# Layers L0 and L1 of a graph network: the sums of a group of edges are taken up one step later, and the ends of a block of nodes spread over the steps after it

## The chip, the cores and the metric

The kernel runs on one core of a Trainium2 chip. The metric is the device time of one execution in microseconds; the profile beside it is of one execution of the same program. TensorE is called PE here (its weight loads PEld), VectorE DVE, ScalarE ACT, GpSimd POOL, and SyncE SP; SP issues most of the plain transfers.

## What is computed

Four graph layers follow each other over the same 6,250 nodes of 256 features and 100,000 edges, which are sorted by their target node. Before each layer the node rows go through a layer norm and a ReLU, and the layer's result is added to the node rows. The two that the change touches, cut to what matters:

```python
def _L0_gnn_ref(x, edge_index, ...):          # attention over edges, 8 heads of 32
    Qh, Kh, Vh = (x @ Wq + bq), (x @ Wk + bk), (x @ Wv + bv)      # each [N, 8, 32]
    s = einsum('nhc,nhc->nh', Qh, Kh) / sqrt(32)
    alpha = leaky_relu(s[src] + s[dst], 0.2)                      # edges and self loops
    e = exp(alpha - segment_max(alpha, dst)[dst])
    a = e / segment_sum(e, dst)[dst]
    attn = segment_sum(Vh[src] * a[:, :, None], dst)
    h = batch_norm(x + attn @ Wo + bo)
    return batch_norm(h + relu(h @ W1 + b1) @ W2 + b2)

def _L1_gnn_ref(x, rbf, dists, edge_index, ...):   # a filter for each edge
    W = (rbf @ W_r2m.T + b_r2m) * (0.5 * (cos(dists * (PI / 5)) + 1))[:, None]
    h = (x @ W_n2m.T + b_n2m) @ W_lin1.T
    agg = segment_sum(h[src] * W, dst)
    return (agg @ W_lin2.T + b_lin2) @ W_m2n.T

h = relu(layernorm(x)); x = x + L0(h)
h = relu(layernorm(x)); x = x + L1(h, edge_attr_32, edge_weight)
h = relu(layernorm(x)); x = x + L2(h, edge_attr_128)
h = relu(layernorm(x)); x = x + L3(h)
```

## The kernel before

Nodes are kept in 49 blocks of 128 (`NB`). Edges come in 98 groups (`G`) of 8 tiles (`J`) of 128, so a group holds 1,024 edges. Each layer first writes a table of node rows to memory (`vt` for L0, `ht1` for L1, `xt2` and `xt3` for L2 and L3); then a loop over the groups gathers, for every edge, the row of its source node. One gather is an indirect transfer of 128 rows, issued by POOL (`gather`, line 130), 8 for each group.

A group's edges end in a window of 128 target nodes, which starts 64 nodes (`HW`) after that of the group before. The segment sum over a group is done on PE: for each of the 8 tiles a one-hot matrix (edge by node of the window, made by DVE from `iota` and `rel`) is multiplied with the weighted rows, and the 8 products are summed in one PSUM tile, `ps_S` (`sum_tiles`, line 681). A block of nodes is touched by up to four windows; `blocks_done(g)` names the block whose last window is that of group g, so it is block b at g = 2b + 2, every second step, and block 48 at the last group, 97.

The four layers are four such loops. Between L0 and L1 stand L0's feed-forward part and the table of L1, from 1226 to 1495 us, without gathers. A gather of L1 needs the whole of `ht1`, and one of L2 the whole of `xt2`.

The order of the work is written out by hand in the parts under `tc.manual_schedule()`: each engine runs its instructions in the order in which the code names them, and an instruction that waits holds up all behind it on its engine.

*L0, step g of the loop at line 818.* The gathers of a group go into one of 6 places in `xbuf` (`NV`) and wait only until PE has summed the group that lay there 6 groups before; the first four groups' gathers are issued ahead of the loop. SP loads `drow` for group g + 2, and `v`, the block's own value rows. Then:

- `sum_block` (line 699) moves the windows of the block that was finished by group g - 1 into place, by 2 to 4 matmuls with shifted unit matrices, in `ps_T` (one buffer). `project0` (line 800) multiplies the block finished by group g - 2 with Wo, in `ps_B` (two buffers).
- `logits0` on DVE (lines 771, 123, 773) adds the target's score to the gathered scores; ACT makes the exponentials (lines 774, 775). `one_hot_t` (line 748, DVE) makes `to`, the one-hot of the next group with nodes on the partitions, from `drow`, and PE uses it in `of_dst` (line 763) to fetch the next group's target scores into `ps_A`. Line 836 (DVE) weights the gathered rows.
- `attn0` (lines 781 to 786, DVE) adds the self loop and divides, for the block in `ps_T`.
- `sum_window` (lines 681 and 691) sums the group on PE, and ACT copies the sum to `ws` at once.
- `turn0` (lines 792, 794) transposes the block on PE, and ACT copies it to `mt`. `one_hot0` (line 754, DVE) makes the next group's 8 one-hots. `residual0` (lines 808, 810, DVE) adds the projected block and takes its statistics for the batch norm, which needs all blocks.

*L1, step g of the loop at line 1005.* The gathers go into one of 12 places in `big` (`NH`). `filters` (line 980, PE) makes the edge filters in three `ps_A` buffers, line 1026 (DVE) multiplies them into the gathered rows, PE sums the window, now with features on the partitions, and DVE and ACT add it to `agg` (lines 1056, 1057) at the end of the same step. Lines 1031 and 1032 (DVE) work out an edge term for L2. For a finished block, line 1015 (PE) projects its 128 columns of `agg`, `out1` (lines 992 to 995, DVE, with the statistics in lines 145 and 146 and ACT's square root in line 126) adds it to the node rows and norms them, line 1022 transposes, ACT applies the ReLU (line 1038), line 1041 multiplies with the weights of L2's table, and lines 1047 to 1049 write the row of `xt2`. Here `ps_B` and `ps_C` have one buffer each, and `ps_S` two.

## Time and profile before

| What | us |
|---|---|
| median of 6 runs (lowest, highest) | 4501.55 (4499.86, 4505.31) |
| the profiled execution, and its span | 4501.5, 4499.7 |
| first gather of L0 to the end of its last | 180.7 to 1201.3 |
| feed-forward of L0 and table of L1 | 1226 to 1495 |
| first gather of L1 to the end of its last | 1495.3 to 2476.0 |
| gathers of L2 | 2495.8 to 3481.1 |
| gathers of L3 | 3502.0 to 4485.2 |
| PE, DVE, ACT, POOL busy over the span | 3079.4, 2103.6, 619.5, 3055.6 |

In the lines of the profile an instruction is named by its line in the kernel, its engine and its operation, and by its tiles (out<-in, with buffer numbers left out; `big<-ht` is a gather of L1, `xbuf<-vt` one of L0, `vg<-xt` one of L2 or L3). A line of the costliest groups ends with busy time and mean ns of one, and the idle time of the engine just before, with what ended it; "issue" is time in which the engine waited for nothing that the profile shows. A line of the waits has the sum in us, the number of times and the longest. A line of the timeline has start, duration and instruction, with the idle time before it in brackets. A line of the stretches has the length, then busy time and number of instructions of PE, PEld, DVE, ACT and POOL, the clock that PE was granted (1.00 is full speed), the share of the DMA engines in use and GB/s. A float32 matmul stands as two records, so 8 matmuls are x16.

### The profile page before, as it was taken

How to read it: one execution, taken by the hardware profiler on the slowest of the kernel's cores; microseconds unless marked ns; L12 is line 12 of the kernel's file. 1: busy time of each engine (PE TensorE's matmuls, PEld its weight loads, DVE VectorE, ACT ScalarE, POOL GpSimd, SP SyncE). 2: the span in 40 equal slices, each digit the busy share in tenths (PEclk: the TensorE clock that was granted, in tenths of full speed). 3: DMA queues.
4: the chain of work that ended last, by engine and by line, in shares of the span. 5: the costliest groups of instructions: out<-in, count | busy, mean ns of one | idle time of the engine just before them, and what ended most of it. 6: DMA issues, size and time to landing. Idle time of an engine off the chain costs nothing. (4 is left out here: it accounts for less than half of the span.)

```text
span 4499.7 us, 42030 instructions
## 1 busy us (share of the span) xinstructions
PE 3079.4 (68%) x12132; PEld 2392.3 (53%) x12133; DVE 2103.6 (47%) x6391; ACT 619.5 (14%) x1559; POOL 3055.6 (68%) x3215
## 2 busy tenths in 40 slices
PE   7788888888797556666666566666666556666655
PEld 4377777777645444555445344545454444444444
DVE  5476665566524566766667333333333222222222
ACT  3211010000124100000000122222222000000000
POOL 0377777777501677777777677777777677777776
PEclk9888888888898777777778788888888788787888
DMA  3365555555500344444444344444443333333333
GB/s 105 112 180 169 161 160 160 162 163 161 154 1 14 110 128 126 122 127 124 128 126 115 90 111 113 113 112 113 112 113 109 96 112 111 112 112 110 112 112 101
DMA packets 258740, 536.78 MB, mean 119 GB/s; under 512 B 65096, under 2 KB 144966, under 8 KB 258502
## 3 DMA queue, kind: packets, MB, share of 16 engines
q0 software_dynamic: 137984, 364.28, 28.6%
q1 hardware_dynamic: 107750, 156.85, 11.4%
q10 hardware_dynamic: 12768, 12.85, 0.9%
q8 instruction: 105, 1.72, 0.2%
q14 instruction: 133, 1.09, 0.1%
HBM read 504.57 MB, written 29.15 MB: 119 GB/s over the span
## 5 line engine op out<-in xcount | busy, mean ns | idle before, releaser
L130 POOL DMA_INDIRECT vg<-xt,src_i x1568 | 1488.7, 949 | 520.4 <-issue 486.7
L681 PE MATMUL ps_S<-vg,oh 128*128 128x258 f32 (+1 forms) x3136 | 986.0, 483 | 782.9 <-DMA vg<-xt,src_i 408.9
L681 PEld LDWEIGHTS ps_S<-vg,oh 128*128 128x128 f32 x3136 | 761.2, 249 | 999.9 <-issue 388.4
L130 POOL DMA_INDIRECT xbuf<-vt,src_i x784 | 782.0, 997 | 241.0 <-issue 211.2
L130 POOL DMA_INDIRECT big<-ht,src_i x784 | 742.1, 947 | 246.3 <-issue 183.8
L681 PE MATMUL ps_S<-oh,big 128*128 128x128 f32 x1568 | 320.9, 388 | 324.1 <-DVE big L1026 260.9
L1150 DVE TENSOR_SCALAR oh<-iota,rel 128x128 f32<-128x128 f32 x784 | 166.5, 302 | 742.5 <-PE ps_S L681 739.3
L681 PE MATMUL ps_S<-xbuf,oh 128*128 128x265 f32 x1568 | 489.8, 478 | 13.7 <-issue 13.4
L681 PEld LDWEIGHTS ps_S<-oh,big 128*128 128x128 f32 x1568 | 298.1, 292 | 354.7 <-DVE big L1026 235.2
L681 PEld LDWEIGHTS ps_S<-xbuf,oh 128*128 128x128 f32 x1568 | 369.5, 242 | 101.0 <-issue 17.4
L763 PE MATMUL ps_A<-scw,to 128*128 128x16 f32 x1568 | 223.7, 286 | 112.1 <-DVE to L748 111.9
L763 PEld LDWEIGHTS ps_A<-scw,to 128*128 128x128 f32 x1568 | 220.2, 223 | 131.2 <-issue 80.8
L1095 DVE TENSOR_SCALAR oh<-iota,rel,ex 128x128 f32<-128x128 f32 x784 | 215.1, 368 | 139.1 <-ACT ex L1092 139.1
L699 PE MATMUL ps_T<-ws,shifts 128*128 128x265 f32 (+2 forms) x1164 | 278.7, 382 | 0.0
L691 ACT ACTIVATE ws<-ps_S 128x265 f32<-128x265 f32 (+1 forms) x196 | 76.5, 390 | 1221.6 <-PE ps_S L681 1221.6
L699 PEld LDWEIGHTS ps_T<-ws,shifts 128*128 128x128 f32 x1164 | 220.8, 190 | 33.7
L836 DVE TENSOR_TENSOR xbuf<-xbuf,ps_E 128x2048 f32<-128x2048 f32 x98 | 223.6, 2282 | 23.7 <-ACT ps_E L774 23.7
L1026 DVE TENSOR_TENSOR big<-big,ps_A 128x384 f32<-128x384 f32 (+1 forms) x294 | 132.3, 505 | 215.2 <-DMA big<-ht,src_i 213.3
L980 PE MATMUL ps_A<-wr,rb 99*128 99x384 f32 (+1 forms) x588 | 215.7, 507 | 9.5 <-DMA rb<-in_rbf 9.5
L1088 DVE TENSOR_TENSOR al<-vg,te 128x8 f32<-128x8 f32 x98 | 16.4, 168 | 432.8 <-DMA vg<-xt,src_i 432.8
L988 DVE TENSOR_SCALAR oh<-iota,rel,cut 128x128 f32<-128x128 f32 x784 | 211.7, 362 | 0.0
L900 POOL TENSOR_TENSOR xbuf<-xbuf,bout 128x1024 f32<-128x1024 f32 (+1 forms) x13 | 29.0, 2228 | 257.5 <-ACT xn L898 250.7
(226 smaller groups left out, 3053.7 us busy)
## 6 DMA issues: line engine op xcount, KB each, us to landing
drow<-in_dst_row SPq DMA_DIRECT2D x98, 512.0 KB
ea<-in_edge_attr SPq DMA_DIRECT2D x98, 512.0 KB
vg<-xt,src_i POOLq DMA_INDIRECT x1568, 2.8
xbuf<-vt,src_i POOLq DMA_INDIRECT x784, 2.9
big<-ht,src_i POOLq DMA_INDIRECT x784, 2.5
rb<-in_rbf SPq DMA_DIRECT2D x196, 49.5 KB
vt<-row SPq DMA_DIRECT2D x49, 132.5 KB
xt<-row SPq DMA_DIRECT2D x49, 129.0 KB
```

Source lines behind the costliest of these rows:

```text
L130: return nc.gpsimd.indirect_dma_start(out=rows, out_offset=None, in_=table, in_offset=bass.IndirectOffsetOnAxis(ap=idx[:, j:j + 1], axis=0))
L681: m = wait_for(nc.tensor.matmul(s, l, r, start=j == 0, stop=j == len(pairs) - 1), made)
L691: nc.scalar.activation(ws, s, AF.Copy)
L699: nc.tensor.matmul(t, shift_by(s), sums[g], start=i == 0, stop=i == len(parts) - 1)
L763: nc.tensor.matmul(dgs[g][:, j, :], tos[g][:, j * P:(j + 1) * P], scw[:, g // 2, g % 2, :], start=True, stop=True)
L836: made_g = nc.vector.tensor_tensor(vals, vals, ex[:, :, :, None].to_broadcast([P, J, H, HD]), OP.mult)
L900: nc.gpsimd.tensor_tensor(x[:, b0:b1, :], x[:, b0:b1, :], w1["bout"][:, None, :].to_broadcast([P, b1 - b0, D]), OP.add)
L980: filtered[g] = nc.tensor.matmul(t, rbs[g][0:33 * n, g % 2, q, :], wr3[0:33 * n, 0:n, :], start=True, stop=True)
L988: nc.vector.tensor_scalar(ohs[g][:, j, :], iota, rel[:, c], w1["cut"][:, c], OP.is_equal, OP.mult)
L1026: made_g = nc.vector.tensor_tensor(hg[:, js, :], hg[:, js, :], t, OP.mult)
L1095: made_g = nc.vector.tensor_scalar(oh[:, j, :], iota, rel[:, g * J + j:g * J + j + 1], ex[:, j:j + 1], OP.is_equal, OP.mult)
L1150: made_g = nc.vector.tensor_scalar(oh[:, j, :], iota, rel[:, g * J + j:g * J + j + 1], None, OP.is_equal)
```

## The change

In both loops, ACT and DVE take up the PSUM sum of group g - 1 in step g (`wins` holds it until then) and no longer that of group g in the same step. The work of a finished block is spread: in L0 `sum_block` runs in the step after the block's last group, behind that step's sums, `attn0` and `turn0` one step later, the copy to `mt` and `project0` one after that, and `residual0` one more; before, `sum_block`, `attn0`, `turn0` and its copy stood in one step, `project0` and `residual0` in the next. In L1 the projection stands in the first step, `out1` and the transposes in the second, the ReLU and the row matmuls in the third, and the row's last addition and write in the fourth; before, the projection and `out1` stood in one step and all the rest in the next. L1's `filters` for the next group move ahead of the group's sums, and its one-hots ahead of the update of `agg` and of the edge term. L1's one-hots get a third buffer and `xn` a second. The loops run three steps more, in which only block work is left. No instruction is added or taken away beside the extra waits that follow from the order.

```diff
@@ -734,7 +734,8 @@
             place = ep.tile([P, G], F32, name="place", bufs=1)
             nc.gpsimd.iota(place, pattern=[[HW, G]], base=-OFF, channel_multiplier=1,
                            allow_small_or_imprecise_dtypes=True)
-            sums, drows, tos, dgs, ohs, mades, vs, ms, mts = {}, {}, {}, {}, {}, {}, {}, {}, {}
+            sums, drows, tos, dgs, ohs, vs, ms, mts = {}, {}, {}, {}, {}, {}, {}, {}
+            wins, blocks, turned, projected = {}, {}, {}, {}
 
             def loads0(g):
                 if g < G:
@@ -751,9 +752,8 @@
                 if g < G:
                     ohs[g] = ep.tile([P, J, P], F32, name="oh")
                     for j in range(J):
-                        mades[g] = nc.vector.tensor_scalar(ohs[g][:, j, :], iota,
-                                                           rel[:, g * J + j:g * J + j + 1],
-                                                           None, OP.is_equal)
+                        nc.vector.tensor_scalar(ohs[g][:, j, :], iota, rel[:, g * J + j:g * J + j + 1],
+                                                None, OP.is_equal)
 
             def of_dst(g):
 
@@ -790,8 +790,7 @@
                 t = ps("B", [P, 2, P])
                 for k in range(2):
                     nc.tensor.transpose(t[:, k, :], mf[:, k * P:(k + 1) * P], ident)
-                mts[b] = ep.tile([P, 2, P], F32, name="mt", bufs=1)
-                nc.scalar.activation(mts[b], t, AF.Copy)
+                return t
 
             def project0(b):
                 t = ps("B", [P, 2, P])
@@ -815,7 +814,7 @@
                 one_hot_t(0)
                 one_hot0(0)
                 of_dst(0)
-                for g in range(G + 2):
+                for g in range(G + 5):
                     vg = vrows[g % NV]
                     if AHEAD <= g < G:
                         rows0(g)
@@ -827,24 +826,34 @@
                         made(of1)
                     if g == 8:
                         made(of2)
-                    summed = [(b, sum_block(sums, b, VR)) for b in blocks_done(g - 1)]
-                    projected = [(b, project0(b)) for b in blocks_done(g - 2)]
                     if g < G:
                         ex = logits0(g)
                         one_hot_t(g + 1)
                         vals = vg[:, :, 0:D].rearrange("p j (h c) -> p j h c", c=HD)
                         made_g = nc.vector.tensor_tensor(
                             vals, vals, ex[:, :, :, None].to_broadcast([P, J, H, HD]), OP.mult)
+                    if 1 <= g <= G:
+                        sums[g - 1] = ep.tile([P, VR], F32, name="ws", bufs=6)
+                        nc.scalar.activation(sums[g - 1], wins.pop(g - 1), AF.Copy)
                     of_dst(g + 1)
-                    for b, s in summed:
-                        attn0(b, s)
                     if g < G:
-                        sums[g], summed0[g] = sum_window(ep, ohs[g], vg, VR, made_g, landed[g])
-                    for b, s in summed:
-                        turn0(b)
+                        wins[g] = ps("S", [P, VR])
+                        summed0[g] = sum_tiles(wins[g], [(ohs[g][:, j, :], vg[:, j, :]) for j in range(J)],
+                                               made_g, landed[g])
+                    for b in blocks_done(g - 2):
+                        attn0(b, blocks.pop(b))
                     one_hot0(g + 1)
-                    for b, t in projected:
-                        residual0(b, t)
+                    for b in blocks_done(g - 4):
+                        residual0(b, projected.pop(b))
+                    for b in blocks_done(g - 3):
+                        mts[b] = ep.tile([P, 2, P], F32, name="mt", bufs=1)
+                        nc.scalar.activation(mts[b], turned.pop(b), AF.Copy)
+                    for b in blocks_done(g - 1):
+                        blocks[b] = sum_block(sums, b, VR)
+                    for b in blocks_done(g - 2):
+                        turned[b] = turn0(b)
+                    for b in blocks_done(g - 3):
+                        projected[b] = project0(b)
             inv_sqrt(dinv, deg, ones_c)
 
 
@@ -958,6 +967,7 @@
 
             agg = ep.tile([P, HW * (G - 1) + P], F32, name="agg", bufs=1)
             rbs, eas, ohs, parts, filtered, summed1, normed = {}, {}, {}, {}, {}, {}, {}
+            wins, added, turned, hbs, rows = {}, {}, {}, {}, {}
 
             def loads(g):
 
@@ -982,7 +992,7 @@
                     parts[g].append((slice(3 * q, 3 * q + n), t))
 
             def one_hot1(g):
-                ohs[g] = ep.tile([P, J, P], F32, name="oh")
+                ohs[g] = ep.tile([P, J, P], F32, name="oh", bufs=3)
                 for j in range(J):
                     c = slice(g * J + j, g * J + j + 1)
                     nc.vector.tensor_scalar(ohs[g][:, j, :], iota, rel[:, c], w1["cut"][:, c],
@@ -991,7 +1001,7 @@
             def out1(b, t):
                 nc.vector.tensor_tensor(x[:, b, :], x[:, b, :], t, OP.add)
                 norm_stats(b, b + 1)
-                xn = ep.tile([P, D], F32, name="xn", bufs=1)
+                xn = ep.tile([P, D], F32, name="xn")
                 nc.vector.tensor_scalar(xn, x[:, b, :], mv[:, b, 0:1], rstd[:, b, :], OP.subtract, OP.mult)
                 return xn
 
@@ -1002,59 +1012,58 @@
                     loads(g)
                 filters(0)
                 one_hot1(0)
-                for g in range(G + 2):
+                for g in range(G + 5):
                     hg = hgs[g % NH]
                     if g < G:
                         got = [wait_for(gather(hg[:, j, :], ht1, src_i[:, g * J:(g + 1) * J], j),
                                         *([summed1[g - NH]] if g >= NH else []))
                                for j in range(J)]
                     loads(g + 2)
-                    added = []
-                    for b in blocks_done(g - 1):
-                        t = ps("B", [P, D])
-                        nc.tensor.matmul(t, agg[:, OFF + b * P:OFF + (b + 1) * P], w1["out"],
-                                         start=True, stop=True)
-                        added.append((b, t))
-                    turned = []
-                    for b in blocks_done(g - 2):
-                        t = ps("B", [P, 2, P])
-                        for k in range(2):
-                            nc.tensor.transpose(t[:, k, :], normed[b][:, k * P:(k + 1) * P], ident)
-                        turned.append((b, t))
                     if g < G:
                         for i, (js, t) in enumerate(parts[g]):
                             made_g = nc.vector.tensor_tensor(hg[:, js, :], hg[:, js, :], t, OP.mult)
                             wait_for(made_g, filtered[g], *(() if i else got))
-                        s = ps("S", [P, P])
-                        summed1[g] = sum_tiles(s, [(hg[:, j, :], ohs[g][:, j, :]) for j in range(J)], made_g, got)
+                    if g + 1 < G:
+                        filters(g + 1)
+                    if g < G:
+                        wins[g] = ps("S", [P, P])
+                        summed1[g] = sum_tiles(wins[g], [(hg[:, j, :], ohs[g][:, j, :]) for j in range(J)],
+                                               made_g, got)
+                    if g + 1 < G:
+                        one_hot1(g + 1)
+                    if 1 <= g <= G:
+                        s = wins.pop(g - 1)
+                        old = HW if g > 1 else 0
+                        c = HW * (g - 1)
+                        if old:
+                            nc.vector.tensor_tensor(agg[:, c:c + old], agg[:, c:c + old], s[:, 0:old], OP.add)
+                        nc.scalar.activation(agg[:, c + old:c + P], s[:, old:P], AF.Copy)
+                    if g < G:
                         ea = eas[g]
                         nc.vector.tensor_tensor(ea, ea, wa[:, None, :].to_broadcast([P, J, FL]), OP.mult)
                         nc.vector.tensor_reduce(te[:, g * J:(g + 1) * J], ea, AX.X, OP.add)
-                    for b, t in added:
-                        normed[b] = out1(b, t)
-                    rows = []
-                    for b, t in turned:
-                        hb = ep.tile([P, 2, P], F32, name="hb", bufs=1)
-                        nc.scalar.activation(hb, t, AF.Relu)
-                        r = ps("C", [P, TR])
-                        for k in range(2):
-                            nc.tensor.matmul(r, hb[:, k, :], w2[0][:, k, :], start=k == 0, stop=k == 1)
-                        rows.append((b, r))
-                    if g + 1 < G:
-                        filters(g + 1)
-                    for b, r in rows:
+                    for b in blocks_done(g - 2):
+                        normed[b] = out1(b, added.pop(b))
+                    for b in blocks_done(g - 4):
                         row = ep.tile([P, TR], F32, name="row2")
-                        nc.vector.tensor_tensor(row, r, w2[1], OP.add)
+                        nc.vector.tensor_tensor(row, rows.pop(b), w2[1], OP.add)
                         nc.scalar.activation(sa[:, b:b + 1], row[:, D:D + 1], AF.Copy)
                         nc.sync.dma_start(xt2[b * P:(b + 1) * P, :], row)
-                    if g + 1 < G:
-                        one_hot1(g + 1)
-                    if g < G:
-                        old = HW if g else 0
-                        c = HW * g
-                        if old:
-                            nc.vector.tensor_tensor(agg[:, c:c + old], agg[:, c:c + old], s[:, 0:old], OP.add)
-                        nc.scalar.activation(agg[:, c + old:c + P], s[:, old:P], AF.Copy)
+                    for b in blocks_done(g - 3):
+                        hbs[b] = ep.tile([P, 2, P], F32, name="hb", bufs=1)
+                        nc.scalar.activation(hbs[b], turned.pop(b), AF.Relu)
+                    for b in blocks_done(g - 1):
+                        added[b] = ps("B", [P, D])
+                        nc.tensor.matmul(added[b], agg[:, OFF + b * P:OFF + (b + 1) * P], w1["out"],
+                                         start=True, stop=True)
+                    for b in blocks_done(g - 2):
+                        turned[b] = ps("B", [P, 2, P])
+                        for k in range(2):
+                            nc.tensor.transpose(turned[b][:, k, :], normed[b][:, k * P:(k + 1) * P], ident)
+                    for b in blocks_done(g - 3):
+                        rows[b] = ps("C", [P, TR])
+                        for k in range(2):
+                            nc.tensor.matmul(rows[b], hbs[b][:, k, :], w2[0][:, k, :], start=k == 0, stop=k == 1)
             nc.vector.tensor_scalar(te, te, w1["ba"], None, OP.add)
 
 
```

## The prediction

> **What bounds the kernel now.** I read the costliest groups first, then the busy times by stage, then the waits, and last the timeline at the places that these pointed to. The groups show one row four times over: POOL issues 8 indirect gathers for each of 98 groups in each of the four layers, 3136 in all.
>
> ```profile
> L130 POOL DMA_INDIRECT vg<-xt,src_i x1568 | 1488.7, 949 | 520.4 <-issue 486.7
> L130 POOL DMA_INDIRECT xbuf<-vt,src_i x784 | 782.0, 997 | 241.0 <-issue 211.2
> L130 POOL DMA_INDIRECT big<-ht,src_i x784 | 742.1, 947 | 246.3 <-issue 183.8
> ```
>
> In L0 (xbuf) the idle time before a gather is 241.0/784 = 0.31 us, in L1 (big) 246.3/784 = 0.31: the 0.30 us between two gathers that a timeline shows each time, and hardly anything beside it. POOL waits for nobody; it needs 0.95 + 0.30 = 1.25 us a gather, 10.0 us a group. So 784 gathers take 784 x 1.25 = 980 us, which is what L1's stage takes (982 us from 1495 to 2477); L0's takes 1022 (180 to 1202). The busy times of these stages and of the two stretches behind them, in which POOL has no gather left:
>
> ```profile
> core 0: us, PE busy (x) PEld busy (x) DVE busy (x) ACT busy (x) POOL busy (x), PEclk, DMA share, GB/s
> 180.00:1202.00 1022.00, 858.26 (x4009) 718.40 (x4010) 621.20 (x1723) 99.46 (x341) 782.23 (x785) 0.83 0.56 168
> 1202.00:1226.00 24.00, 15.34 (x66) 12.16 (x66) 12.81 (x36) 4.42 (x11) 0.00 (x0) 0.86 0.45 148
> 1495.00:2477.00 982.00, 605.89 (x2518) 478.94 (x2518) 665.33 (x1648) 58.93 (x238) 742.06 (x784) 0.78 0.44 125
> 2477.00:2496.00 19.00, 10.52 (x33) 6.97 (x33) 10.99 (x28) 1.76 (x7) 0.20 (x1) 0.65 0.05 15
> ```
>
> PE is busy 84% in L0 and 62% in L1, DVE 61% and 68%: neither is full. The waits say the same: the consumers' first instruction of a step waits for the gather to land (two rows, one each of the waits within L0 and within L1):
>
> ```profile
> DVE al L771 <- DMA xbuf<-vt,src_i: 260.9, 66, 6.5
> ```
>
> ```profile
> DVE big L1026 <- DMA big<-ht,src_i: 198.5, 71, 5.8
> ```
>
> L0's 40 us over 980 are in one place, as a step's timeline shows:
>
> ```profile
> 701.18 0.95 POOL L130 DMA_INDIRECT xbuf<-vt,src_i  x1 [0.30 <-issue]
> 701.55 0.22 DVE L771 TENSOR_TENSOR al<-xbuf,ps_A 128x64 f32<-128x64 f32 x1 [4.15 <-DMA xbuf<-vt,src_i]
> 702.20 0.75 DVE L748 TENSOR_SCALAR to<-drow,place 128x1024 f32<-128x1024 int32 x1
> 702.43 1.34 POOL L130 DMA_INDIRECT xbuf<-vt,src_i  x1 [0.30 <-DVE al L773]
> 704.07 0.95 POOL L130 DMA_INDIRECT xbuf<-vt,src_i  x1 [0.30 <-issue]
> ```
>
> The gather that starts 0.23 us after L748 takes 1.34 instead of 0.95 us. From about 350 us on, when the consumers have caught up with the gathers, this happens in nearly every step, because L748 stands a fixed 0.65 us behind the landing: 0.4 us a step, some 80 steps, over 30 us.
>
> **The change, part by part.**
>
> *Steady steps of L0.* The same instructions run, in other places. ACT's copy of a group's sums (L691, 0.39 us) goes behind the next group's exponentials; sum_block, attn0, turn0, its copy, project0 and residual0 of a block run one or two steps later. All is hidden as long as a pair of steps fits in POOL's time for two, 2 x 10.45 = 20.9 us. PE at full clock, from the timeline around 700 us: twice (of_dst 1.85 + sums 3.83) + sum_block 1.95 + transposes 0.38 + project0 1.16 = 14.85 us; at the stage's granted 0.83 that is 17.9. DVE: attn0 (1.4 us) and residual0 (1.25) now fall into the same step, behind 0.65 + 0.75 + 2.28 + 1.65 us: 8.0 us of one step, 5.3 of the other, each under 10.4. The stalls that go (project0 waited 24.1 us in all for ACT's copy of the transposes, by the waits of this stage) were PE's, while POOL went on. So 0 us. If the cover were gone, the dearer engine would be PE, as a rival below.
>
> *Queues.* POOL: no gather is moved; a gather waits for the sums of six groups before (twelve in L1), which PE still ends in their own step. SP: the load of v needs a buffer that attn0 reads, so it is issued about 4 us later in every second step; behind it stands drow for a later group, which is loaded two steps ahead. In L1 the row writes of a block go out two steps later, behind the same loads. 0 us, while loads are a step ahead (10 us); bounds 0 and 1.
>
> *L748 and the gathers.* L771, L123, L773 and L748 keep their order and still come straight behind the landing, so L748's distance to the next gather should stay near 0.2 us and the 0.4 us a step too. I take 0. The bounds come from the steps of this trace: started 0.13 us ahead of a gather it makes it 1.46 us (at 221 us), 0.51 instead of 0.4, 80 steps +9 us; started 0.05 us ahead (733.71, gather 733.76) the gather takes 0.94, 80 steps -33 us.
>
> *Weights at step 6.* The block's projection now still holds one of the two ps_B buffers while nine small products are made through them. The nearest row is PE's one wait there for DVE (4.9 us, longest); at 0 to 0.5 us for each, 0 to 4.5 us. The gathers are some three groups ahead at 270 us: 0 us.
>
> *Steady steps of L1.* filters move ahead of the sums, the one-hots ahead of L1031, agg's update a step back. DVE's pair of steps stays 2 x (1.35 + 2.14 + 0.22 + 2.43) + 2.05 + 0.43 = 14.8 us of 20.0. 0 us; no gather of L1 is stretched (mean 947 ns), so there is nothing to win.
>
> *The end of L0.* Here nothing covers: the gathers are over. Before, the last group's sums end at about 1214.5 and its block's residual starts so:
>
> ```profile
> 1219.80 0.35 DVE L808 SCALAR_TENSOR_TENSOR big<-ps_B,l_gnn_bo,big 128x128 f32<-128x128 f32 x1 [1.12 <-PE ps_B L800]
> ```
>
> Block 48 (the last) keeps its chain, but block 47 is now a step later, so its work stands in front of it. From 1214.4: sum_block of 47 1.95 (1216.3), project0 of 46 1.05 (1217.4); one ps_T buffer, so sum_block of 48 waits for attn0 of 47 (1.4 behind 1216.3: 1217.7) and takes 1.3 (1219.1); residual of 46 (to 1218.95) is out of the way; attn0 of 48 1.45 (1220.6); transposes 0.4 (1221.05); project0 of 47, which stands behind them, 1.1 (1222.2); residual of 47 1.25 (1223.4); then that of 48. 1223.4 - 1219.8 = +3.6 us. Bounds: 0 if the inserted work slips into gaps; +8 with PE's part (7.3 us) at twice the time, as the half-speed sums at 1201.83 (5.88 us) show.
>
> *The end of L1.* The same with ps_B at one buffer. Before, the sums end at 2482.9 and the next layer's first gather follows at
>
> ```profile
> 2495.80 0.94 POOL L130 DMA_INDIRECT vg<-xt,src_i  x1 [19.75 <-issue]
> ```
>
> Now: matmuls of 47 (0.67) and row matmuls of 46 (2.09, the half-speed duration this stretch shows) to 2485.6; out1 of 47 to 2486.0, row 46 to 2486.4, out1 of 48 to 2488.6; transposes of 47 only when out1 of 48 has read ps_B (2487.0), its copy 2488.2; transposes of 48 to 2489.3; row matmuls of 47 2491.4; row add, sa, copy of 48 to 2492.6; row matmuls 2494.7; row add 2495.1; write and landing 3.1 as before: 2498.2, so +2.4 us. Bounds +0 and +5.
>
> *Sum.* 4501.5 (the profiled execution; its span is 4499.7, the 1.8 us around it stay) + 3.6 + 2.4 = 4507.5 us. The median of the six runs is 4501.55, so both have the same base.
>
> [...] In every second step PE's work now ends at about 7.9 us and the next starts at 11.8: an idle stretch of 3.9 us. Before it was 2.6 to 3.6 (waits for L748), at a granted 0.83. [...]
>
> **The rivals.** *1. The lock slips (faster).* If L748 starts 0.15 us later behind the landing, it misses the gather. For: the margin is small, one step in the trace shows it. Against: in the other locked steps the distance held within 0.1 us, and no instruction before it changes. 4507.5 - 33 = 4474; in every second step alone, 4491. *2. PE becomes the bound of L0 (slower).* Uneven steps drop the clock; it decides from a granted clock of 14.85/20.9 = 0.71. For: L1 was granted 0.78 at 62% busy. Against: a slower PE is idle less. At 0.65: 14.85/0.65 = 22.85, 49 x 1.95 = 96 us, 4604. *3. The ends cost nothing* because the inserted work fits into waits: 4501.5. For: PE idles there (15.3 busy of 24 us). Against: the single ps_T and ps_B buffers tie the two blocks together.
>
> **How the numbers follow.** Forecast 0.62, rival 1 0.15, rival 2 0.07, rival 3 0.16. The time is the forecast's, 4507.5; its own range is 4502 to 4515 (ends 0 to +13 us). With half slips below and a dearer end above, 4490 to 4517 leaves out rival 1 in full and rival 2. About 0.2% (9 us: 4492.5 to 4510.5) is what a measurement of this kernel can tell from no change. Of the forecast, 0.37 lies within and 0.25 above; with rival 3, 0.53 within; above 0.25 + 0.07 = 0.32; below 0.15.
>
> **What would show it.** The gathers of L0 should span 1020 us again and those of L1 981, at means of 997 and 947 ns; from the last gather of L0 to the first aggregate of the batch norm there should be 3.6 us more than 19.9, and 22.2 instead of 19.75 us of idle time before the first gather of L2. The forecast is wrong if L0's mean gather falls to 0.95 (rival 1), if gathers wait for PE's sums (rival 2), or if the two ends stay as they were (rival 3).

## The result, and the profile after

The changed kernel takes 4512.63 us in the median of 19 runs (4507.84 to 4517.1), the kernel before 4501.94 in 39 runs (4499.27 to 4507.88): a ratio of 1.0022, 95% interval 1.0016 to 1.0029. That is about 10.7 us more, 5 us above the forecast of 4507.5 and inside its range. The profiled execution took 4512.12 us, its span 4510.4.

Nine of the twelve runs below fell into times in which every kernel is some 16% slower (the kernel before at 5210 to 5253 us); they are called the late runs, because TensorE's results come late in them (last section), and each ratio is against the kernel before run together with it.

The groups of the page after, by line, engine, operation and tiles, count, busy us, mean ns, and idle time before with its main releaser:

```profile
span 4510.4 us, 42124 instructions
...
L130 POOL DMA_INDIRECT xbuf<-vt,src_i x784 | 784.2, 1000 | 241.0 <-issue 209.4
L130 POOL DMA_INDIRECT big<-ht,src_i x784 | 744.7, 950 | 246.4 <-issue 163.4
...
L1024 DVE TENSOR_TENSOR big<-big,ps_A 128x384 f32<-128x384 f32 (+1 forms) x294 | 132.3, 505 | 300.3 <-DMA big<-ht,src_i 299.8
```

The last of these rows in the kernel before:

```profile
L1026 DVE TENSOR_TENSOR big<-big,ps_A 128x384 f32<-128x384 f32 (+1 forms) x294 | 132.3, 505 | 215.2 <-DMA big<-ht,src_i 213.3
```

POOL's idle time is what it was, 0.31 us a gather: in the steady steps no gather waits for a consumer in either kernel. The gathers of L0 and L1 are 3 ns longer each in the mean. VectorE's product in L1 (L1024, L1026 before) waits 299.8 us for gathers to land, 213.3 before: the consumers are quicker to be ready, as the change is meant to make them, and wait longer for the same stream.

Cut at the first and last gather of each layer, the two profiled executions differ so:

| Stretch (us) | before | after | difference | forecast |
|---|---|---|---|---|
| L0, first gather to the end of the last | 1020.58 | 1022.84 | +2.26 | 0 |
| from there to L1's first gather | 294.06 | 297.69 | +3.63 | +3.6 |
| L1, first gather to the end of the last | 980.74 | 983.37 | +2.63 | 0 |
| from there to L2's first gather | 19.75 | 20.79 | +1.04 | +2.4 |
| L2, L3 and what lies around them | 2184.6 | 2185.7 | +1.1 | 0 |

The first line is 784 gathers of 1.25 us (980 us) and the time over 0.945 us that they take: 41.1 us before, 43.3 after. The stretched gather is in the timeline after, in nearly every step (start, duration, engine, line, idle time before):

```profile
703.23 0.75 DVE L749 TENSOR_SCALAR to<-drow,place 128x1024 f32<-128x1024 int32 x1
703.38 1.41 POOL L130 DMA_INDIRECT xbuf<-vt,src_i  x1 [0.30 <-DVE al L773]
```

The comparison starts 0.15 us ahead, the gather takes 1.41 us. L0's end in the timeline after:

```profile
1202.20 0.95 POOL L130 DMA_INDIRECT xbuf<-vt,src_i  x1 [0.30 <-issue]
...
1222.56 0.35 DVE L807 SCALAR_TENSOR_TENSOR big<-ps_B,l_gnn_bo,big 128x128 f32<-128x128 f32 x1 [1.43 <-PE ps_B L799]
1222.62 0.38 ACT L850 ACTIVATE mt<-ps_B 128x256 f32<-128x256 f32 x1 [0.57 <-PE ps_B L799]
...
1223.05 1.16 PE L799 MATMUL ps_B<-mt,l_gnn_wo 128*128 128x128 f32 x8 [0.53 <-ACT mt L850]
...
1224.25 0.35 DVE L807 SCALAR_TENSOR_TENSOR big<-ps_B,l_gnn_bo,big 128x128 f32<-128x128 f32 x1 [0.24 <-PE ps_B L799]
...
1225.07 1.47 DVE L429 BATCH_NORM_AGGREGATE mb<-st 128x2 f32<-128x294 f32 x1
...
1229.55 2.93 ACT L446 ACTIVATE hn<-big,sh,rs 128x512 f32<-128x512 f32 x4 [1.03 <-DVE sh L433]
```

The same two places in the kernel before, whose last gather ends at 1201.25:

```profile
1221.13 2.80 DVE L429 BATCH_NORM_AGGREGATE mb<-st 128x2 f32<-128x294 f32 x2
...
1225.23 2.93 ACT L446 ACTIVATE hn<-big,sh,rs 128x512 f32<-128x512 f32 x4 [0.98 <-DVE sh L433]
```

The residual of block 47 (1222.56) stands in front of that of block 48 (1224.25), the last work before the batch norm's aggregate. But it is not VectorE that holds block 48 up: VectorE waits 0.24 us for PE's projection of block 48 (1223.05), which waits for ACT's copy to `mt` (1222.62), and this for PE's projection of block 47, since `mt` has one buffer. The aggregate starts 21.92 us after the last gather's end (1203.15), 19.87 before, and ScalarE's L446 behind it 26.41 us after (23.98 before).

A step of L1 in the timeline after:

```profile
2003.91 1.35 DVE L1024 TENSOR_TENSOR big<-big,ps_A 128x384 f32<-128x384 f32 x3 [1.59 <-DMA big<-ht,src_i]
...
2005.18 2.23 DVE L998 TENSOR_SCALAR oh<-iota,rel,cut 128x128 f32<-128x128 f32 x8
...
2006.33 1.03 POOL L130 DMA_INDIRECT big<-ht,src_i  x1 [0.30 <-issue]
```

The product starts on the landing in 97 of 98 steps now (73 before), the one-hots 1.27 us behind its start in every step (3.65 to 7.31 us before), and a gather that starts in the middle of these eight short instructions takes 1.03 us. In L1 37 gathers are over 1.0 us, 11 before, and all 37 start during one-hots; the sum over 0.945 us is 3.83 us, 1.18 before: this is the +2.6. End of L1:

```profile
2504.99 0.94 POOL L130 DMA_INDIRECT vg<-xt,src_i  x1 [20.79 <-issue]
```

### The profile page after: what moved, and what is told of

The parts are those of the page before. It is cut to its first block, busy times and chain, and to the rows that moved or that the text cites. A ratio compares the mean times of both kernels' runs of the same rounds, so it can differ in the third digit from the quotient of the medians.

```text
span 4510.4 us, 42124 instructions
## 1 busy us (share of the span) xinstructions
PE 3080.2 (68%) x12132; PEld 2390.5 (53%) x12133; DVE 2099.8 (47%) x6391; ACT 612.2 (14%) x1559; POOL 3061.0 (68%) x3215
## 3 DMA queue, kind: packets, MB, share of 16 engines
q1 hardware_dynamic: 107750, 156.85, 11.4%
## 5 line engine op out<-in xcount | busy, mean ns | idle before, releaser
L681 PE MATMUL ps_S<-xbuf,oh 128*128 128x265 f32 x1568 | 468.5, 462 | 7.3 <-DVE xbuf L833 3.9
L990 PE MATMUL ps_A<-wr,rb 99*128 99x384 f32 (+1 forms) x588 | 294.3, 657 | 221.5 <-DVE big L1024 210.6
L681 PEld LDWEIGHTS ps_S<-xbuf,oh 128*128 128x128 f32 x1568 | 355.5, 233 | 84.8 <-issue 8.5
L763 PE MATMUL ps_A<-scw,to 128*128 128x16 f32 x1568 | 236.0, 295 | 172.3 <-DVE to L749 172.2
L763 PEld LDWEIGHTS ps_A<-scw,to 128*128 128x128 f32 x1568 | 232.7, 235 | 182.9 <-issue 152.3
L990 PEld LDWEIGHTS ps_A<-wr,rb 99*128 99x128 f32 (+1 forms) x588 | 145.9, 265 | 345.8 <-DVE big L1024 268.5
L681 PEld LDWEIGHTS ps_S<-oh,big 128*128 128x128 f32 x1568 | 277.1, 265 | 17.0 <-issue 3.8
L681 PE MATMUL ps_S<-oh,big 128*128 128x128 f32 x1568 | 270.3, 345 | 3.4 <-DVE big L1024 3.4
L1024 DVE TENSOR_TENSOR big<-big,ps_A 128x384 f32<-128x384 f32 (+1 forms) x294 | 132.3, 505 | 300.3 <-DMA big<-ht,src_i 299.8
L1097 DVE TENSOR_TENSOR al<-vg,te 128x8 f32<-128x8 f32 x98 | 16.4, 167 | 426.6 <-DMA vg<-xt,src_i 426.6
```

What stands on the lines that cost most here:

```text
L681: m = wait_for(nc.tensor.matmul(s, l, r, start=j == 0, stop=j == len(pairs) - 1), made)
L763: nc.tensor.matmul(dgs[g][:, j, :], tos[g][:, j * P:(j + 1) * P], scw[:, g // 2, g % 2, :], start=True, stop=True)
L990: filtered[g] = nc.tensor.matmul(t, rbs[g][0:33 * n, g % 2, q, :], wr3[0:33 * n, 0:n, :], start=True, stop=True)
L1024: made_g = nc.vector.tensor_tensor(hg[:, js, :], hg[:, js, :], t, OP.mult)
L1097: nc.vector.tensor_tensor(al[:, :, None], vgs[g][:, :, D:D + 1], te[:, gs][:, :, None], OP.add)
```

## The experiments

**One loop alone.** L0's loop of the changed kernel with L1's of the kernel before, and the other way round.

```diff
--- the changed kernel
-                for g in range(G + 5):
-                    hg = hgs[g % NH]
...
+                for g in range(G + 2):
+                    hg = hgs[g % NH]
...
```

> The new loop of L0 with the old loop of L1. My theory: the changed kernel's extra time is a sum of four places, and this kernel has the two that lie in L0: the stretch from L0's first gather to its last is 1022.8 us as in the changed kernel (1020.6 before, +2.3) and the stretch from there to L1's first gather 297.7 (294.1 before, +3.6), while L1's gathers span 980.7 and the gap to L2 19.75 as before; +5.9 us in all, ratio about 1.0013. Rival (the prediction's own sum: only the ends cost): L0's gathers span 1020.6 again, +3.6 us. Rival (the two loops act on each other, for instance over the clock): L1's span is not 980.7.

> The old loop of L0 with the new loop of L1. My theory: L1's gathers span 983.4 us as in the changed kernel (980.7 before, +2.6) and the gap from L1's last gather to L2's first is 20.8 (19.75 before, +1.0); L0's 1020.6 and the 294.1 after it as before; +3.7 us, ratio about 1.0008. Rival (the prediction's sum): L1's span 980.7 and the gap 22.2, +2.4 us.

Both were late runs. L0 alone: 5248.82 us, ratio 1.0006 (0.9995 to 1.0017). L1 alone: 5218.28 us, ratio 0.995 (0.9933 to 0.9966): 0.5% faster, where +0.08% was expected. From L1's first gather to L2's first it took 1208.1 us with the new loop and 1232.8 with the old one, 0.25 us a step. In L0 the new loop's gathers span 1200.7 us, 6.8 less than with the old one, and the stretch to L1 329.1, 12.3 more. (L2, which is the same code in both, differs by 7.6 us, so the 6.8 us are not read here.) The waits in L1 from 1900 to 2600 us say what the new loop is for (engine, tile and line, releaser, us in total, times, longest). With the old loop:

```profile
PE ps_S L681 <- DVE big L1035: 215.4, 31, 9.9
```

and with the new one, in the unaltered changed kernel's late run:

```profile
PE ps_B L1062 <- DVE xn L1005: 132.1, 31, 5.8
```

TensorE no longer waits for the product, because VectorE does it before it takes up the last sums. Most of the 215 us comes back as other waits, the row above and idle time without a recorded wait before the sums (164 us, 42 with the old loop); what is left is time of the whole kernel here, where the consumers and not POOL set the pace. My additive theory was one of the normal pace, and these runs couldn't test it.

**The comparison for `to`, three ways.** First it was moved behind the product, in both kernels:

```diff
                         ex = logits0(g)
-                        one_hot_t(g + 1)
                         vals = vg[:, :, 0:D].rearrange("p j (h c) -> p j h c", c=HD)
                         made_g = nc.vector.tensor_tensor(
                             vals, vals, ex[:, :, :, None].to_broadcast([P, J, H, HD]), OP.mult)
+                        one_hot_t(g + 1)
```

> The changed kernel, with L0's comparison that writes the tile `to` moved on VectorE to behind the 128x2048 product of the step; nothing else moves. Theory (the lock): a comparison that starts 0.1 to 0.6 us ahead of a gather makes this gather 1.3 to 1.5 us long instead of 0.94, one in nearly each of L0's steps, 35 us in all, and this paces L0, not its consumers. Behind the product, the comparison no longer starts just ahead of the second gather, so L0's gathers span about 988 us (980 to 1000) instead of 1022.8, and the kernel is about 33 us faster than the changed one, 4479 us. If it falls just ahead of another gather instead, the span stays at 1020. Rival (consumers pace L0: TensorE with its 0.81 clock, or VectorE's chain): the long gathers go, but the gathers wait instead, and the span stays above 1010.

> The same move of the one comparison in the kernel before. Theory (the lock): L0's gathers span 980 to 1000 us instead of 1020.6, about 4468 us in all. It tells whether the gain needs the change: if consumers that take a result in its own step can't follow a faster stream of gathers, the span falls less here than in the changed kernel (rival: by at least 10 us less); if TensorE's wait for the results is hidden anyway, it falls by the same amount, within 5 us.

Late runs again: 5272.06 us, ratio 1.0058 (1.0041 to 1.0075), and 5301.8, ratio 1.0112 (1.0094 to 1.0129). In the changed kernel the gathers' sum over 0.945 us fell from 26.9 us (L0 alone, run together with it) to 16.5, but the time from L0's first gather to L1's first rose from 1529.8 to 1570.7, 0.4 us a step. In the kernel before the sum did not even fall (28.7 us; the old loop of L0 has 24.6 in the run with L1 alone). The comparison now stands in front of `of_dst` and the next step's logits, which is the likely price where consumers set the pace; no run separates it. As a way to shorten L0 the move failed here; the normal pace was not tried.

Second, another form of the instruction in the old place. L1's edge term, a tensor_tensor of the same 128x1024, takes 1.22 us where the comparison takes 0.75, and stretches no gather (-1 ns in the mean of 95, table below). My theory was that the form decides, so that a tensor_tensor here would leave the gathers at 0.95 us:

```diff
-                    nc.vector.tensor_scalar(tos[g], drows[g], place[:, g:g + 1], None, OP.is_equal)
+                    nc.vector.tensor_tensor(tos[g], drows[g], place[:, g:g + 1].to_broadcast([P, J * P]),
+                                            OP.is_equal)
```

> The changed kernel with the same comparison for `to` in the same place, written as a tensor_tensor against the broadcast column instead of a tensor_scalar; nothing else. [...] About 33 us less than the changed kernel (4479 where that takes 4512). Rival (any long VectorE instruction in this place does it): the gathers stay at 1.3 to 1.5 us, and the longer comparison makes them 0.4 us longer still. Rival (consumers pace L0): the gathers are short but wait for sums, and the span stays above 1010 us.

Ratio 0.9989 (0.9977 to 1.0), late. My theory fell on the gathers themselves, and the first rival was right; the timeline of this run:

```profile
740.72 1.22 DVE L749 TENSOR_TENSOR to<-drow,place 128x1024 f32<-128x1024 int32 x1
740.93 1.83 POOL L130 DMA_INDIRECT xbuf<-vt,src_i  x1 [3.28 <-issue]
```

The 87 gathers that started during the comparison ended 0.81 us after its end in the mean, as with the tensor_scalar (0.80), so they got longer with it: the sum over 0.945 us is 61.7 us. So it isn't the form. VectorE's larger groups, sorted by whether gathers that start during them are stretched (trace of before; L0 and L1), gave the next theory:

| VectorE instruction | inputs | gathers begun during it | mean, longest stretch (ns) |
|---|---|---|---|
| L748 `to`, 128x1024 | SBUF | 89 | 380, 512 |
| L754, L988 one-hots, 128x128 | SBUF | 306, 224 | 30, 127 and 8, 120 |
| L995 `xn`, 128x256 | SBUF | 15 | 22, 131 |
| L836 product, 128x2048 | SBUF and PSUM | 119 | 0, 10 |
| L1031 edge term, 128x1024 | SBUF and PSUM | 95 | -1, 2 |
| L1032 reduction, 128x1024 | one SBUF | 95 | -2, 3 |

The last row says more than the theory does: all operands of L1032 lie in SBUF, and it stretches nothing. It has one input, the stretching ones have two in SBUF.

Third, then, the column `place` was put into PSUM, into the bank of `ps_E`:

```diff
+            pe = ps("E", [P, J * H + G])
+            placed = pe[:, J * H:J * H + G]
+            nc.vector.tensor_copy(placed, place)
...
-                ex = ps("E", [P, J, H])
+                ex = pe[:, 0:J * H].rearrange("p (j h) -> p j h", j=J)
...
-                    nc.vector.tensor_scalar(tos[g], drows[g], place[:, g:g + 1], None, OP.is_equal)
+                    nc.vector.tensor_tensor(tos[g], drows[g], placed[:, g:g + 1].to_broadcast([P, J * P]),
+                                            OP.is_equal)
```

> The changed kernel, with the comparison for `to` as a tensor_tensor in its place, whose second input, the column `place`, lies in PSUM (in the bank of ps_E) instead of SBUF; the same numbers, nothing else. Theory (an instruction of VectorE stretches a gather only where all its operands lie in SBUF; the instructions with a ps_ operand stretch none in any layer): no gather that starts during the comparison is longer than 0.96 us, where the tensor_scalar made it end 0.82 us after the comparison's end (1.3 to 1.5 us long) and the tensor_tensor with both inputs in SBUF too (1.5 to 1.9 us). The sum over 0.945 us in L0 falls below 8 us (43 in the changed kernel's trace at 4510 us, 62 with the SBUF tensor_tensor). Where POOL sets the pace this is 35 us of L0's span; where the sums are waited for, the span changes by less than 15 us. Rival (the length of the instruction or its place behind the landing decides): gathers of 1.5 to 1.9 us again.

Ratio 0.9978 (0.9968 to 0.9988), late, beside 0.9974 (0.9964 to 0.9984) of the changed kernel run together with it. None of the 86 gathers that started during the comparison was stretched by more than 4 ns; L0's sum over 0.945 us is 5.0 us, 24.4 in the changed kernel there. L0's gathers span 1188.2 us, 1184.7 there: as expected, short gathers are worth nothing where sums are waited for. The run with the tensor_tensor and this one differ in where one input lies, so that this decides is shown; its price needed the normal pace, below.

**The changed kernel again.**

> The changed kernel itself, unaltered, to have its time and trace under the conditions of the experiments. Theory (what the change is worth depends on how late TensorE's results come): where the kernel before takes about 5245 us and VectorE and POOL resume several us after the matmuls they wait for, the effects of the two loops add up from their single runs, 1.0006 x 0.995 = ratio 0.9956, with the stretch from L0's last gather to L1's first at about 329 us (316.8 with the old loop) and the gap from L1's last gather to L2's first at about 83 us (102 with the old loop). Where the kernel before takes 4502 us, ratio 1.0022 again, with 297.7 and 20.8 us. Rival (the change costs the same 10 us everywhere): 1.002 in both.

Late: 5195.34 us, ratio 0.9974 (0.9964 to 0.9984), so faster by a quarter of a per cent, where the result was slower by 0.22%. The sum of the two loops, 0.9956, lies outside the interval; the stretch to L1 is 327.1 us and the gap to L2 82.2, as expected. What the change is worth has a different sign in the two conditions.

**The loop ends put back.** The last two steps of both loops in the order of the kernel before.

```diff
-                for g in range(G + 5):
+                for g in range(G - 1):
                     vg = vrows[g % NV]
...
+                copied0(G - 2)
+                for g in range(G - 1, G + 2):
...
+                    for b in blocks_done(g - 1):
+                        blocks[b] = sum_block(sums, b, VR)
...
+                    for b in late:
+                        projected[b] = project0(b)
+                    if g < G:
+                        ex = logits0(g)
...
```

> The changed kernel, with the last two steps of L0's and of L1's loop in the order of the kernel before: block 47 is summed at the start of step 97 and goes through within it, only block 48 comes after. All steps up to 95 are the changed kernel's. Theory (the ends cost what block 47, one step late, puts in front of block 48): the stretch from L0's last gather to L1's first falls from 297.7 to 294.1 us (-3.6) and the gap from L1's last gather to L2's first from 20.8 to 19.75 (-1.0), while L0's and L1's gathers span 1022.8 and 983.4 as in the changed kernel: 4.6 us less than it. Rival (the late sums of the steady steps cost it, TensorE still being behind when the gathers end): both gaps stay.

> The changed kernel with the last two steps of both loops in the order of the kernel before, once more, for conditions in which the kernel before takes 4502 us. Theory (L0's end costs 3.6 us, because block 47 stands in front of block 48): the stretch from L0's last gather to L1's first falls from 297.7 to 294.1 us or below, L0's gathers span 1022.8 us as in the changed kernel, the gap from L1's last gather to L2's first is 19.2 to 21.3 us as in all kernels so far, and the median is 3.6 to 5 us under the changed kernel's 4512.6: 4508, ratio 1.0013. L1's gathers, whose code up to step 95 is the changed kernel's, tell whether their 983.4 us belong to the early one-hots (983.4 again) or to chance (980.7 to 982.2, as in the other four traces). Rival (the end is as dear in any order): 297.7 again, ratio 1.0022.

Both were late: ratio 0.9955 (0.9938 to 0.9972) and 0.9967 (0.9955 to 0.998). In the first, L446 of the feed-forward starts 42.9 us after L0's last gather, in the run beside it with the new ends 58.7 (that one has the longer comparison too); in the second 52.6, beside 47.5 with the old loop and 52.2 to 59.0 in the late runs with the new ends. That points to new ends that cost more where results come late, but the two figures lie 9.7 us apart and the ranges touch, so how much is open, and the 3.6 us of the normal pace wasn't measured by this kernel alone. Both intervals overlap that of the changed kernel's 0.9974. The gap between L1 and L2 did not move (83.9 and 83.8).

**At the normal pace.** The next three runs had it. One kernel puts the ends back and reads `place` from PSUM, one has only the latter, on the kernel before:

> The changed kernel with the two parts that the runs so far name as its costs or as a cost of both kernels put right: the loop ends in the order of the kernel before (as in the run with old ends), and the comparison for `to` reading `place` from PSUM (as in the run that took the stretch out of the gathers). Theory (the parts add up): where the kernel before takes 5200 to 5250 us, 0.9974 of the changed kernel less about 14 us for L0's end and 3 for the comparison, ratio 0.994 (0.993 to 0.996); where it takes 4502 us, 35 us less of gathers and 4.6 of ends, 4473 us, ratio 0.9936. No gather of L0 that starts during the comparison is over 0.96 us. Rival (the earlier end of block 47 in L0 was a matter of the chip that ran it): ratio 0.997.

> The kernel before with nothing but the comparison for `to` reading `place` from PSUM. Theory: where POOL sets the pace (kernel before at 4502 us) L0's gathers span 986 us instead of 1020.6 and the kernel takes 4467 us, ratio 0.992, so that the change isn't needed for that gain; where the kernel before takes 5200 to 5250 us, consumers set the pace, the comparison is 0.45 us longer on their chain and the gathers shorter for nothing: ratio 0.998 to 1.002. Rival (the long gathers hold the consumers up there too): ratio under 0.996.

4471.28 us (4468.79 to 4472.7), ratio 0.9932 (0.9916 to 0.9949), against an expected 4473; and 4480.89 us (4480.47 to 4487.73), ratio 0.9955 (0.9939 to 0.9972), against an expected 4467. The first beats both kernels. Its sum was met by luck in the parts: against the changed kernel L0's gathers gave 30.0 us, not 35, and the stretch to L1 7.0, not 3.6. L0's gathers span 992.8 and 1004.2 us, and their sums over 0.945 us are 8.2 and 6.9 us, so the stretch is gone in both. What the second lacks is in POOL's waits from 180 to 400 us. The kernel before with `place` in PSUM:

```profile
POOL xbuf L130 <- ACT xbuf L779: 17.8, 6, 9.9
```

The changed kernel with `place` in PSUM and the old ends:

```profile
POOL xbuf L130 <- ACT ws L841: 2.5, 1, 2.5
POOL xbuf L130 <- ACT mt L854: 1.4, 1, 1.4
```

And the longest of the six waits, in the timeline of the former, with the step before it:

```profile
304.05 1.22 DVE L751 TENSOR_TENSOR to<-drow,ps_E 128x1024 f32<-128x1024 int32 x1 [1.63 <-ACT ps_E L778]
...
305.33 3.60 PE L767 MATMUL ps_A<-scw,to 128*128 128x16 f32 x16 [1.48 <-DVE to L751]
...
315.22 0.39 ACT L691 ACTIVATE ws<-ps_S 128x265 f32<-128x265 f32 x1 [11.03 <-PE ps_S L681]
315.51 0.22 ACT L778 ACTIVATE ps_E<-al 128x64 f32<-128x64 f32 x1
315.66 0.25 ACT L779 ACTIVATE xbuf<-al 128x64 f32<-128x64 f32 x1
315.77 1.22 DVE L751 TENSOR_TENSOR to<-drow,ps_E 128x1024 f32<-128x1024 int32 x1 [4.72 <-ACT ps_E L778]
...
315.93 0.94 POOL L130 DMA_INDIRECT xbuf<-vt,src_i  x1 [9.85 <-ACT xbuf L779]
```

The gather belongs to group 12 and waits for PE's sum of group 6, which lay in its place and ends at 315.2; it starts 0.75 us behind that sum's end, in the other kernel too, where no exponential ended near, so the releaser named is only the one that happened to end then. PE is late because of the experiment's own edit. The comparison shares a tile with the exponentials and waits for them (4.72 us at 315.77; 1.4 us in the mean from 400 to 1150 us, 0.36 in the other kernel), the exponentials stand behind ACT's copy of the last sums, this waits for PE, and PE's `of_dst` waits for the comparison. So from one of the first six groups' sums to the next it takes 9.8 us, where it is 5.9 in the changed order, whose copy stands behind the exponentials. The kernel before itself has no such ring: its comparison waits for nobody, the first sums follow each other in 7.0 us, and that of group 6 is done 13 us before its place is needed (304.0):

```profile
285.03 5.20 PE L681 MATMUL ps_S<-xbuf,oh 128*128 128x265 f32 x16
```

By the medians the changed order with its ends put back is 9.6 us faster here (4480.89 - 4471.28), by the two traces 11.4 us in L0's span, and the waits account for it (12.7 us more of them, 1.3 us less of stretch). That is the price of a wait which reading `place` from the bank of the exponentials brought in. What the change is worth with short gathers and without that wait, say with `place` in a bank of its own, was not run.

**One part of L1 undone**, run together with these:

```diff
-                    if g + 1 < G:
-                        one_hot1(g + 1)
                     if 1 <= g <= G:
                         s = wins.pop(g - 1)
...
+                    if g + 1 < G:
+                        one_hot1(g + 1)
                     for b in blocks_done(g - 3):
                         hbs[b] = ep.tile([P, 2, P], F32, name="hb", bufs=1)
```

> The changed kernel with one part of L1's change undone: the one-hots of the next group stand on VectorE behind the edge term, the block's normalisation and its row again, instead of straight behind the product; the sums of a group are still taken up one step later. Theory (late taking up, not the early one-hots, is what the change brings where TensorE's results come late): from L1's first gather to L2's first it takes as long as in the changed kernel (1199 us on the chip that ran it, 1208 to 1212 on others, against 1233 with the old loop), ratio 0.9974 within 0.0015. Where POOL sets the pace (kernel before at 4502 us), L1's gathers span 981 instead of 983.4 us, 2.4 us less than the changed kernel. Rival (the early one-hots bring it, since TensorE's sums wait for them): at least half of the 24 us of L1 is lost again, ratio 0.9995 or more.

4509.86 us, ratio 1.0017 (1.0008 to 1.0027), beside 1.0022 (1.0016 to 1.0029) of the changed kernel: not told apart. L1's gathers span 982.16 us, between the 980.74 before and the 983.37 after; 17 of them are over 1.0 us. But the kernel above with ends and `place` put right has the early one-hots and spans 981.47 (20 over 1.0 us), and the kernel before with `place` in PSUM, whose loop of L1 is not touched at all, has the late ones and spans 981.40 (18 over 1.0 us). So the place of the one-hots in the code doesn't settle it: what counts is how they fall against the gathers, and that differs from kernel to kernel. This kernel also repeats L0 of the changed kernel unaltered: 1022.84 us and 297.70 us to L1, the same figures as in the result's trace. Its other question, which part of the change to L1 pays where results come late, stays untested, since it ran at the normal pace.

## Why the prediction held, and where it didn't

The total came out inside its range, but not by its own parts: of the 10.7 us between the two traces 6.0 lie where the sum had nothing (L0's and L1's gathers, L2 and L3), and the two ends gave 4.7 instead of 6.0. The range was made for half slips and dearer ends, so that it held these is luck.

*POOL bounds the kernel, and steady steps gain nothing.* Right at the pace of the result: the gathers wait for nobody in either trace, and the quicker consumers wait longer for the landing.

*L748 and the gathers, taken as 0 between +9 and -33.* Inside its bounds, and mis-sized by +2.26 us: the gathers begun during the comparison are 35.1 us over 0.945 in sum where they were 33.9, as it stands at a slightly worse distance, and all others 8.2 us where they were 7.2. Rival 1, the slip, didn't happen by itself. Taking the cause away brought nearly what its price said, 30 us of L0's span, 1022.8 to 992.8, in the kernel with the change, and 16.4 in the one without it, where the remedy brought its own wait. The cause that I had implied, a comparison too close to a gather, was incomplete: the distance costs something only with both its inputs in SBUF, and with `place` in PSUM none of 86 gathers was stretched by more than 4 ns.

*The end of L0, +3.6.* The sum was met (+3.63), partly by luck. From the end of the last sums on PE to the residual of block 48 it took 9.5 us instead of 5.3, so 4.2 more and not 3.6, and the wait in it was PE's projection behind the one `mt` buffer, not the residual of block 47 that the working has. The sums themselves ended 11.6 us after the last gather instead of 13.3, which the working did not have. So the first aggregate, the sign that the prediction named, came 2.05 us later and L446 2.4; the other 1.2 us lie in the feed-forward, whose code is the same and which took 268.1 to 271.3 us from L446 to L1's first gather in all runs, for no known reason. With the ends put back and `place` in PSUM, L446 came 22.55 us after the last gather, 3.9 us sooner than in the changed kernel.

*The steady steps of L1, 0: "no gather of L1 is stretched (mean 947 ns), so there is nothing to win".* This is the step that missed most, +2.63 us. It asked what could be won and not what could be lost: VectorE's work now starts on the landing in nearly every step, as L0's does, so the one-hots can fall into the same fixed distance to a gather. The gathers over 1.0 us, all of them during one-hots, show that in this trace. The size is open: at the normal pace the changed loop cost 2.6 us here and 0.7 in another kernel, 1.4 with the one-hots put back, and the untouched loop 0.7 in another trace.

*The end of L1, +2.4.* Mis-sized: +1.04. The row matmuls took 1.13 and 1.04 us for two of the three blocks, not the half-speed 2.09 that I used for all; only the last took 2.09. And kernels with the old ends gave 19.75, 20.47 and 21.34 us, with the new ones 20.79 and 19.24, so one microsecond is not told from nothing here.

*Idle stretches and the clock.* The sum has nothing for PE's idle stretches, 3.9 us in every second step by the working, and rightly: L0's steady steps were granted 0.83 in both kernels. Single stretches do show in the clock. From 350 to 1190 us the granted clock, by its records in the traces, fell to half 59 times before and 41 times after, for 287 us in all each time. It came in all 20 idle gaps of PE's matmuls over 2 us before, or within 2 us of their end (gaps of 2.1 to 3.6 us), and with 34 of the 38 after (2.4 to 6.0 us, 3.8 in the median). So the longer gaps were there as worked out, and the steps' mean clock was no lower for them.

*Rival 2, TensorE as the bound makes the change slower.* Not tested as it stands: in the late runs consumers do set the pace, but the clock granted in L0 (200 to 1350 us) was 0.76 to 0.77, not below the 0.71 (14.85 us of PE's work in 20.9 us) at which I let it decide. There L0's new loop alone made no difference (1.0006), and with L1's the changed kernel is the faster one, 0.9974. I had charged the lower clock to the changed kernel alone, and its price should have been compared with what the same clock does to the kernel before. *Rival 3, free ends,* is ruled out for L0: 297.7 us in two traces with the new ends, 290.7 to 294.1 in three with the old.

## What to carry to other kernels

Making consumers quicker behind a queue that sets the pace moves their idle time and nothing else (in L1 from 213.3 to 299.8 us of waits for gathers), and the first and last steps, which nothing covers, then pay for the longer pipeline (3.63 us behind L0's gathers); look first for what stretches the queue's own instructions. A remedy that makes an instruction wait for another engine has a price of its own, which depends on the order around it (9.6 us between the two kernels with `place` in PSUM): look in the trace for the wait that the edit added before reading the rest of the difference. An instruction that starts a fixed time after a landing keeps nearly the same distance to the queue's next instruction in every step, so one bad distance can be paid in most of them (81 gathers of L0's 98 steps were stretched by 0.2 to 0.5 us): this holds for work that the change moves there as well. Before a rival gets a price, work it out for both kernels.

## What the runs showed of the hardware

*A VectorE instruction with two inputs in SBUF can hold up a gather that starts during it until it ends.* A gather that starts 0.1 to 0.5 us after the start of such an instruction ends 0.81 to 0.84 us after its end, whatever its own start: 0.75 us of tensor_scalar makes it 1.1 to 1.5 us long (81 gathers each before and after), 1.22 us of tensor_tensor 1.6 to 1.9 (36 gathers). With one input in PSUM, 95 gathers begun during the same 1.22 us took 0.94 to 0.96 us:

```profile
703.40 1.22 DVE L752 TENSOR_TENSOR to<-drow,ps_E 128x1024 f32<-128x1024 int32 x1 [0.35 <-ACT ps_E L778]
704.41 0.95 POOL L130 DMA_INDIRECT xbuf<-vt,src_i  x1 [0.30 <-issue]
```

In the mean the tensor_scalar stretches a gather begun during it by 0.38 us (89 gathers before), the tensor_tensor by 0.61 (87 gathers). What in the gather is held up, and by what, no run tells.

*In the late runs TensorE's instructions come singly, with no wait recorded, and its results arrive late.* A stretch of L1 in the changed kernel's late run:

```profile
2402.75 1.28 PE L681 MATMUL ps_S<-oh,big 128*128 128x128 f32 x10
...
2404.71 0.27 PE L681 MATMUL ps_S<-oh,big 128*128 128x128 f32 x1 [0.68 <-issue]
...
2406.12 0.27 PE L681 MATMUL ps_S<-oh,big 128*128 128x128 f32 x1 [1.14 <-issue]
...
2408.23 0.27 PE L681 MATMUL ps_S<-oh,big 128*128 128x128 f32 x1 [1.84 <-issue]
...
2411.17 0.22 DVE L1039 TENSOR_TENSOR agg<-agg,ps_S 128x64 f32<-128x64 f32 x1 [8.84 <-remote]
2411.34 0.94 POOL L130 DMA_INDIRECT big<-ht,src_i  x1 [3.20 <-remote]
```

VectorE's L1039 takes up the sum of the group before, whose matmuls end at 2399.89 by their records, and the gather waits for the same sum to free its place. Both go on at 2411.2 and 2411.3, 11 us later; at the normal pace a gather that waited started 0.75 us behind the sum's end. Of the next sum, ten of the 16 records run in 1.28 us, and the other six spread from 2404.71 to 2411.81. It happens while gathers run: those of the four layers span 1185, 1117, 1120 and 1109 us in this run, 1023, 983, 986 and 984 in the result's trace, while the feed-forward takes 271 us in both. It came on four chips, one of which gave the normal 4501 us another time. What brings it about stays open; none of these runs tells.
